# A shorter look-ahead for GpSimd's row fetches in a sparse two-layer graph kernel

## The chip, the cores and the metric

The kernel runs on one NeuronCore of a Trainium2 chip. The metric is the device time of one execution in microseconds. Engines are named as in the profile: PE is TensorE, DVE is VectorE, ACT is ScalarE, POOL is GpSimd, SP is the queue that issues plain DMAs.

## What is computed

Two graph layers over 2708 nodes with 512 features. `adj` is sparse (about 0.3% of its entries are set, values between 0.05 and 1) and has a nonzero diagonal.

```python
# layer 0
rowsum = adj.sum(axis=1)
d = where(rowsum > 0, rowsum ** -0.5, 0)
out = relu((d[:, None] * adj * d[None, :]) @ x @ W + b)
h = layernorm(x + out)
# layer 1
xn = h @ W_node + b_node
feats = einsum('nd,hdf->hnf', xn, K)          # 4 heads
logits = s[:, :, None] - 1e10 * (1 - adj)     # s: one number for each row and head
out = relu(mean over heads of softmax(logits) @ feats)
y = layernorm(h + out)
```

In layer 1 the factor 1e10 makes the softmax pick one column, that of the row's largest entry. So layer 1 needs, for row i, one row of `u = h @ M + c`, where `M` is the mean over heads of `W_node @ K`: the row of the largest entry of `adj[i]`. Rows where that would not hold exactly raise a flag, and a dense path stands behind the flag.

## The kernel before, in words

**Blocks and chunks.** Rows go in blocks of 128 (`NB` = 22; `NS` = 21 are whole). A first stage loads `adj`, sums its rows on ACT, finds the largest entries of each third of a row on DVE, and stores the scaled products `v = d * (x @ W)` to DRAM as `v_d`. The main loop then goes over blocks `ib` 0 to 20 and in each over `C` = 9 chunks `c`, with `n = 9 * ib + c`. Each chunk needs 128 rows of `v_d`, gathered by an indirect DMA of 256 KB that GpSimd issues (`fetch_chunk`, `fetch`, line 611). In chunks 0, 3 and 6 of a block the gathered rows are the rows' own largest entries of one third; in blocks 1 to 20 DVE adds them in (`add_chunk`, line 662). The other six chunks hold the rest of the entries in packed lists (`lists[ib]`, computed one block or more ahead by `hot`, `enlist` and `listed`), and PE adds them with a small 128x128 matrix (line 672).

**Order of work.** The schedule is by hand (`manual_schedule`): each engine does its instructions in the order in which the program writes them, and waits on semaphores only where data or buffers are not ready. So an instruction written earlier or later matters only by what it then stands before or behind on its own engine. Gather buffers are taken from two pools of 12 in turn (`row_space`, lines 617 to 622) once the search has ended, which is in block 8 (`found_at` = 8); so a buffer comes round again 24 gathers later.

**Look-ahead.** Ahead of chunk `n`, `fetch_until(m)` writes the gathers of all chunks below `m` that are not yet written, as far as their lists exist. Line 1151 gives `m`. The list of a block must have been written before its chunks 1, 2, 4, 5, 7 and 8 can be gathered; `fetch_until` stops at the first block without a list.

**The tail that is mixed in.** `norm_1` (lines 711 and 712, then `squares`, line 721) ends a block; its normalised rows `h` are turned on PE (`turn_h`), multiplied by `M` (`u_product`, line 235), read from PSUM by DVE into `ut` (line 790) and stored as `u`. Rows below 2304 (`EARLY` = 18 blocks) go to `u_e`, those of blocks 0 to 16 by a plain store on SP; block 17 by a scatter from GpSimd that leaves out flagged rows (`put`, line 1029, index `put_own`); later blocks by scatters into `u_d`. A few flagged rows are done by a dense sum (`l_a`, `l_v`, `acc_l`), and their product `l_u` is scattered into `u_e` (index `to_put`) and `u_d` (`put_d`) by two more `put`s. These three scatters are written at fixed distances in chunks after the products that they need (`later`).

Four chunks after the last row of `u_e` is written, `pieces_y(1)` follows in three chunks of four: `y_fetch(n)` gathers the selected rows of `u_e` for block n (line 1052, index `idx`), `y_1(n)` adds them to `h` on DVE six pieces later (line 1063, then `squares`), and in groups of three blocks come the root, the last normalisation and the store to `out`. After the main loop come the products of the last two blocks, the other `y` gathers, the rows whose selected row lies in `u_d` (index `top_d`) and their scatters to `out_dram` (line 1029). GpSimd has no other work in the main loop past block 10, except the root of the flagged rows (lines 268 to 271) and their two gathers.

**Where the change lies in the queue.** Among the last instructions on GpSimd of the main loop, in the order before: the gather of chunk (20,0), those of chunks (20,1) to (20,8), then `put` of `l_u` into `u_e`, `put` of block 17's `ut` into `u_e`, `put` of `l_u` into `u_d`, then `y_fetch` 0, 1, 2 and so on.

Of the kernel before, what the change touches and what calls it, by code (L numbers as in the profile page):

```python
# [44 lines left out]
ALU = mybir.AluOpType  # L45
# [18 lines left out]
def tile_two_graph_layers(  # L64
# [11 lines left out]
    nc = tc.nc  # L76
# [11 lines left out]
    def rows(ib):  # L88
        return min(P, N - ib * P)
# [60 lines left out]
    bad_i = const.tile([1, 1], I32, name="bad_i")  # L150
# [234 lines left out]
    def hot(ib):  # L385

        lo = max(g for g in GROUPS if g <= ib)
        ends = starts[lo]
        h_t = search.tile([P, T, 2 * P], BF16, name="hot", bufs=2)
        for t in range(T):  # L390
            past = search.tile([P, 2 * P], BF16, name="past", bufs=2)
            nc.vector.tensor_scalar(past, slots, ends[:, 1, ib - lo, t : t + 1], None, op0=ALU.is_gt)  # L392
            nc.vector.scalar_tensor_tensor(  # L393
                h_t[:, t, :], slots, ends[:, 0, ib - lo, t : t + 1], past, op0=ALU.is_gt, op1=ALU.subtract
            )
        hots[ib] = h_t

    def enlist(ib):
        ls = sheets[ib] = p_one.tile([P, D], F32, name="ls")
        h_t = hots.pop(ib)  # L400
        for k in range(NL):
            nc.tensor.matmul(
                ls[:, k * W_REC : (k + 1) * W_REC],
                h_t[:, k // 2, k % 2 * P : (k % 2 + 1) * P],
                packed[:, ib, k // 2, :],
                start=True,
                stop=True,
            )
# [36 lines left out]
    def search_next():  # L445
        ib, t = finds.pop(0)
        find(ib, t)
        if t == T - 1:
            under_0(ib)
            scanned[0] = ib + 1  # L450
            load_blocks()

    def group(lo):
        hi = GROUPS[GROUPS.index(lo) + 1]
        pack_1(lo, hi)
        pack_2(lo, hi)
        pack_3(lo, hi)
        if hi == NB:
            nc.vector.memset(flag[: N - full, NS:], 1.0)
# [40 lines left out]
    def weights(d):  # L500

        ps = p_po.tile([P, D], F32, name="po")
        for e in range(ND):
            nc.tensor.matmul(ps, wT[:, e, d * P : (d + 1) * P], km[:, e, :], start=(e == 0), stop=(e == ND - 1))
        nc.scalar.copy(m_sb[:, d, :], ps)
# [118 lines left out]
    def fetch_chunk(ib, c):  # L624
        kind, t = CHUNKS[c][:2]
        g = gs[ib, c] = row_space()
        if kind == "d":
            pr = rows(ib)
            fetch(g, pr, cols[:pr, ib, t, CHUNKS[c][2] : CHUNKS[c][2] + 1], v_d[: reach(c), :])
        else:  # L630
            fetch(g, P, lists[ib][0][:, t : t + 1], v_d[: reach(c), :])
# [25 lines left out]
    def add_chunk(ib, c):  # L657
        pr = rows(ib)
        g = gs.pop((ib, c))
        if by_vector(ib, c):  # L660
            vs = own[ib][0]
            nc.vector.scalar_tensor_tensor(  # L662
                vs, g, scaled[:, ib, CHUNKS[c][1], 0:1], vs, op0=ALU.mult, op1=ALU.add
            )
            return
        first = ib not in acc
        if first:
            acc[ib] = p_acc.tile([P, D], F32, name="acc")
            if bias_on_pe(ib):
                start_from(acc[ib], pr, b_3)  # L670
        k = pr if CHUNKS[c][0] == "d" else P
        nc.tensor.matmul(  # L672
            acc[ib][:pr],
            ss.pop((ib, c))[:k, :pr],
            g[:k],
            start=(first and not bias_on_pe(ib)),
            stop=(c == len(CHUNKS) - 1),
        )
# [60 lines left out]
    def root_1(lo, hi):  # L739

        s = slice(lo, hi)
        nc.scalar.activation(sds[:, s], sqs[:, s], AF.Sqrt, scale=1.0 / D, bias=eps_1)
        nc.vector.tensor_scalar(vrs[:, s], sqs[:, s], 1.0 / D, EPS, op0=ALU.mult, op1=ALU.add)
# [67 lines left out]
    def later(chunks_on, f):  # L811
        due.append([chunks_on, f])
# [295 lines left out]
    def fetch_until(n):  # L1108
        while fetched[0] < min(n, len(chunks)) and in_turn[fetched[0]][0] in lists:
            fetch_chunk(*in_turn[fetched[0]])  # L1110
            fetched[0] += 1

    def form_until(n):
        while formed[0] < min(n, len(chunks)) and chunks[formed[0]][0] in lists:
            small_matrix(*chunks[formed[0]])
            formed[0] += 1
# [28 lines left out]
    found_at = None  # L1145
    for ib in range(NS):
        pr = rows(ib)
        for c in range(C):
            n = ib * C + c
            form_until(n + 11)  # L1150
            fetch_until(n + (9 if n < 14 else 11) + (0 if found_at is None else min(11, max(0, 2 * (ib - found_at - 3)))))
            add_chunk(ib, c)
            group_of = max(g for g in GROUPS if g <= hot_next)
            if (
                c in (0, 5)
                and hot_next < NS
                and hot_next <= ib + (2 if c == 0 else 4)
                and group_of in starts
                and not (c == 5 and found_at is not None and ib == found_at + 1)
            ):  # L1160
                hot(hot_next)
                listing[n + 4] = lambda k=hot_next: enlist(k)
                listing[n + 6] = lambda k=hot_next: listed(k)
                hot_next += 1
            if n in listing:
                listing.pop(n)()
            if ib == 0 and c in (5, 8):
                weights(2 if c == 5 else 3)
            if finds and c in ((1, 4, 7) if ib < 3 else (1, 5)):
                search_next()  # L1170
            if c == 2 and not finds and found_at is None:
                group(GROUPS[2])
                searching[0] = False
                found_at = ib
            if found_at is not None:
                for f in plan.pop((ib - found_at, c), []):
                    f()
            if c == 2 and ib > ROOTS_AT:
                root_1(ib - 1, ib)
            if c == (2 if ib <= ROOTS_AT else 3) and ib:  # L1180
                k = slice(ib - 1, ib)
                if ib <= ROOTS_AT:
                    norm_2(ib - 1, ib, rows(ib - 1))
                else:
                    root_2(ib - 1, ib)
                    nc.scalar.activation(nbs[:, k], nms[:, k], AF.Copy, scale=rss[:, k])
                norm_3(ib - 1, rows(ib - 1), space(ib - 1))
                store(h_d, space(ib - 1), ib - 1)
                waiting_h.append(ib - 1)
            if c == (7 if ib < EARLY else 6):  # L1190
                for _ in range(2):
                    if waiting_h:
                        turn_h(waiting_h.pop(0))
            for k in sorted(products_u):
                u_store(k)
            if c == (5 if ib < EARLY else 8 if ib == EARLY else 1) or (ib == EARLY and c == 5):
                for k in sorted(hTs):
                    u_product(k)
            if found_at == ib - 3 and c == 4:
                products_l = list(range(NB))  # L1200
            if c % 2 and products_l:
                listed_turn(products_l.pop(0))
            elif len(dl.get("turned", [])) > (2 if products_l else 0):
                listed_product(dl["turned"].pop(0))
            if dl.get("at") == n - 2:
                root_1(L, L + 1)
                root_2(L, L + 1)
                norm_v(L, P, h_of[L])
                waiting_h.append(L)
            if L in h_of and "at" not in dl:  # L1210
                dl["at"] = n
            if "set" not in dl and u_done >= set(range(EARLY - 1)) | {L}:
                dl["set"] = n
                later(3, lambda: put(dl["u"], u_e[:, :], dl["put"][:, NLATE:], EARLY * P))
                later(5, lambda: put(dl["u"], u_d[:, :], dl["put_d"], N - EARLY * P))
            if "go" not in dl and u_done >= set(range(EARLY)) | {L}:
                dl["go"] = n + 4
            if n >= dl.get("go", n + 1) and (n - dl["go"]) % 4 != 3 and n < len(chunks) - 3:
                pieces_y(1)
            tick()  # L1220
        if not finds and late is None:
# [7 lines left out]
            po = p_po.tile([P, D], F32, name="po")  # L1229
# [13 lines left out]
    ib = NS - 1  # L1243
# [35 lines left out]
    po = p_po.tile([P, D], F32, name="po")  # L1279
# [14 lines left out]
    for n in first:  # L1294
        rows_out(n)
    root_2(second[0], second[-1] + 1)
    nc.vector.tensor_copy(bad_i, po[:1, :1])
    for n in second:
        y_3(n)
        rows_out(n)  # L1300
# [146 lines left out]
```

## Time and profile before

| | |
|---|---|
| time, median of 3 runs | 490.34 us (489.5 to 492.23) |
| the profiled execution's own time | 488.01 us |
| its span in the profile | 486.3 us |
| busy, share of the span: PE, DVE, ACT, POOL | 77%, 81%, 64%, 63% |
| DMA moved | 140.67 MB, mean 289 GB/s |
| gathers of line 611: lists, own entries | 126 at 1010 ns, 63 at 1007 ns |

The time lies 1.7 us above the span, which counts from the first to the last instruction. [...] Times in the views are microseconds from the span's start.

### The profile page before, as it was taken

To read this page: it belongs to the slowest core of one execution; us is meant where nothing else is said; L and a number is where in the kernel's file an instruction comes from. 1 tells how busy PE (TensorE), PEld (TensorE's weight loads), DVE (VectorE), ACT (ScalarE), POOL (GpSimd) and SP (SyncE) were. 2 spreads that over 40 slices of the span, in tenths; PEclk is the share of its full clock that TensorE was granted. 3 is DMA by queue.
4 is the path that set the end of the run, shared out by engine and by line. 5 is a ranking of instruction groups with operands and counts; after the bars stand their busy time and mean duration, and the time that the engine had idled before them with its cause. 6 is when DMAs were issued, how large, how long until landed. Compare 5 with 4: busy or idle time off the path is not lost.

```text
span 486.3 us, 5318 instructions
## 1 busy us (share of the span) xinstructions
PE 376.8 (77%) x1129; PEld 168.8 (35%) x1129; DVE 391.7 (81%) x1079; ACT 312.3 (64%) x575; POOL 305.3 (63%) x434
## 2 busy tenths in 40 slices
PE   4979788788978987799977958699999999880000
PEld 3434344333223333344323423344444444340000
DVE  2799989879799999999999996666667697667661
ACT  1599999797886556776773453865666322348680
POOL 2343544454477677777787577777777665677703
PEclk9998998798997999999999889799999999995555
DMA  7999999998548678889889789999999688469952
GB/s 232 419 398 416 422 339 371 357 336 342 197 119 286 202 235 264 263 253 315 272 258 290 228 261 371 376 325 376 369 367 313 219 270 269 138 194 308 322 193 84
DMA packets 51565, 140.67 MB, mean 289 GB/s; under 512 B 10617, under 2 KB 10617, under 8 KB 48688
## 3 DMA queue, kind: packets, MB, share of 16 engines
q0 software_dynamic: 21840, 68.29, 45.1%
q1 hardware_dynamic: 29684, 71.95, 39.4%
q8 instruction: 11, 0.18, 0.2%
q14 instruction: 30, 0.25, 0.2%
HBM read 117.33 MB, written 24.99 MB: 293 GB/s over the span
## 4 chain that ended last, share of the span: by engine, by line
DVE 28%; PE 19%; DMA 7%; issue 5%; ACT 3%; POOL 3%; POOLq 0%; DVEq 0%; ACTq 0%
PE acc L672 7%; PE po L235 6%; PE acc_l L1012 4%; DVE ats L319 4%; DVE vals L318 3%; DVE hot L393 3%; DVE vs L662 2%; DMA l_a<-in_adj_dram,to_read 2%; DMA g<-u_e,idx 2%; POOL g L611 1%; DVE past L392 1%; DVE h_early L712 1%; DMA g<-v_d,l_col 1%; DVE h_late L1063 1%; DVE vs L711 1%
## 5 line engine op out<-in xcount | busy, mean ns | idle before, releaser
L611 POOL DMA_INDIRECT g<-v_d,l_col x126 | 127.3, 1010 | 42.6 <-issue 22.1
L672 PE MATMUL acc<-g,s 128*128 128x512 f32 x278 | 143.2, 628 | 4.3 <-DMA g<-v_d,l_col 2.6
L235 PE MATMUL acc<-w_sb,sT 128*128 128x512 f32 (+1 forms) x176 | 89.1, 654 | 0.0
L235 PE MATMUL po<-m_sb,sT 128*128 128x512 f32 x176 | 80.8, 603 | 2.7 <-ACT sT L226 2.7
L611 POOL DMA_INDIRECT g<-v_d,cols x63 | 63.4, 1007 | 19.7 <-issue 13.1
L318 DVE MAX8 vals<-a 128x8 f32<-128x896 f32 (+2 forms) x66 | 71.7, 1087 | 2.8 <-ACT a L299 2.8
L319 DVE FIND_INDEX8 ats<-vals,a 128x8 uint32<-128x896 f32 (+2 forms) x66 | 72.1, 1092 | 0.0
L672 PEld LDWEIGHTS acc<-g,s 128*128 128x128 f32 x278 | 49.1, 196 | 50.1 <-issue 42.3
L305 ACT ACTIVATE a<-a 128x2708 f32<-128x2708 f32 (+1 forms) x22 | 54.4, 2471 | 12.4 <-DVE ats L319 12.4
L299 ACT ACTIVATE a<-a 128x2708 f32<-128x2708 f32 (+1 forms) x22 | 54.8, 2490 | 10.0 <-POOL a L311 10.0
L235 PEld LDWEIGHTS po<-m_sb,sT 128*128 128x128 f32 x176 | 33.5, 194 | 45.0 <-issue 38.2
L235 PEld LDWEIGHTS acc<-w_sb,sT 128*128 128x128 f32 (+1 forms) x176 | 34.7, 208 | 38.6 <-issue 38.5
L649 ACT ACTIVATE s<-s,l_val,l_minus 128x128 f32<-128x128 f32 x86 | 42.4, 493 | 2.9
L311 POOL TENSOR_SCALAR_AFFINE_SELECT a<-a 128x128 f32<-128x128 f32 (+1 forms) x22 | 7.2, 327 | 56.0 <-DMA a<-in_adj_dram 49.7
L226 ACT COPY sT<-tp 128x512 f32<-128x512 f32 (+1 forms) x44 | 25.8, 586 | 24.8 <-PE tp L224 24.8
L662 DVE SCALAR_TENSOR_TENSOR vs<-g,scaled,vs 128x512 f32<-128x512 f32 x50 | 37.2, 744 | 0.1
L224 PE MATMUL tp<-ident,x 128*128 128x128 f32 (+1 forms) x88 | 15.4, 303 | 23.6 <-DMA x<-in_x_dram 15.5
L648 ACT ACTIVATE s<-place,l_row 128x128 f32<-128x128 f32 x86 | 33.4, 388 | 0.0
L393 DVE SCALAR_TENSOR_TENSOR hot<-slots,ends,past 128x256 bf16<-128x256 bf16 x63 | 30.6, 485 | 2.2
L1052 POOL DMA_INDIRECT g<-u_e,idx x21 | 21.9, 1041 | 7.1 <-issue 5.5
L726 ACT ACTIVATE nms<-tot 128x1 f32<-128x1 f32 x10 | 2.0, 202 | 34.8 <-DVE h_early L712 19.5
L721 ACT ACTIVATE xr<-h_late,nms 128x512 f32<-128x512 f32 x11 | 7.9, 722 | 24.7 <-DVE nms L720 24.7
(265 smaller groups left out, 579.5 us busy)
## 6 DMA issues: line engine op xcount, KB each, us to landing
a<-in_adj_dram SPq DMA_DIRECT2D x21, 1354.0 KB, 9.3
x<-in_x_dram SPq DMA_DIRECT2D x21, 256.0 KB, 19.1
vs<-v_d SPq DMA_DIRECT2D x21, 256.0 KB, 4.9
xr<-in_x_dram SPq DMA_DIRECT2D x21, 256.0 KB, 5.9
l_v<-v_d SPq DMA_DIRECT2D x21, 256.0 KB, 5.0
u_e<-ut SPq DMA_DIRECT2D x17, 256.0 KB
h_d<-h_late SPq DMA_DIRECT2D x13, 256.0 KB, 2.9
out_dram<-h_late SPq DMA_DIRECT2D x13, 256.0 KB, 4.4
```

What stands on the lines that cost most here:

```text
L226: copy(sT[:, :, :pr], ps[:, :, :pr])
L235: nc.tensor.matmul(po[:pr], sT[:, f, :pr], wt[:, f, :], start=(f == 0 and row_3 is None), stop=(f == ND - 1))
L299: nc.scalar.activation(a, a, AF.Copy, accum_out=sums[:pr, ib : ib + 1])
L305: nc.scalar.activation(a, a, AF.Relu, scale=-1.0, accum_out=bad[:pr, NB + ib : NB + ib + 1])
L318: nc.vector.max(out=vals[:pr, ib, t, :], in_=part)
L319: nc.vector.max_index(out=ats[:pr, ib, t, :], in_max=vals[:pr, ib, t, :], in_values=part)
L393: nc.vector.scalar_tensor_tensor(h_t[:, t, :], slots, ends[:, 0, ib - lo, t : t + 1], past, op0=ALU.is_gt, op1=ALU.subtract)
L611: nc.gpsimd.indirect_dma_start(out=t[:pr], out_offset=None, in_=src, in_offset=bass.IndirectOffsetOnAxis(ap=ap, axis=0))
L648: nc.scalar.activation(s[:, :pr], place[:, :pr], AF.Abs, bias=minus_row[:, t : t + 1])
L649: nc.scalar.activation(s[:, :pr], s[:, :pr], AF.Relu, scale=minus_val[:, t : t + 1], bias=val[:, t : t + 1])
L662: nc.vector.scalar_tensor_tensor(vs, g, scaled[:, ib, CHUNKS[c][1], 0:1], vs, op0=ALU.mult, op1=ALU.add)
L672: nc.tensor.matmul(acc[ib][:pr], ss.pop((ib, c))[:k, :pr], g[:k], start=(first and not bias_on_pe(ib)), stop=(c == len(CHUNKS) - 1),)
```

## The change

Line 1151 no longer adds the term that grows with the block. With `found_at` = 8 it was 0 up to block 11, 2 in block 12, 4 in block 13 and so on up to 11, so that the nominal distance went from 11 to 22 chunks; what was really written ahead, because of the lists, was 16 to 22 chunks in blocks 16 to 18. Now it is 11 chunks everywhere. A second edit at line 1297 makes the flag by a comparison where it was a copy with a conversion; it is one operation on one element in both.

```diff
@@ -1148,7 +1148,7 @@
         for c in range(C):
             n = ib * C + c
             form_until(n + 11)
-            fetch_until(n + (9 if n < 14 else 11) + (0 if found_at is None else min(11, max(0, 2 * (ib - found_at - 3)))))
+            fetch_until(n + (9 if n < 14 else 11))
             add_chunk(ib, c)
@@ -1294,7 +1294,7 @@
     root_2(second[0], second[-1] + 1)
-    nc.vector.tensor_copy(bad_i, po[:1, :1])
+    nc.vector.tensor_scalar(bad_i, po[:1, :1], 0.0, None, op0=ALU.is_gt)
     for n in second:
```

The instructions of PE, DVE, ACT and SP keep their order. On GpSimd the order is the same up to the gather of chunk (20,0). From there it is:

```
before: (20,1) ... (20,8)   put l_u->u_e   put ut->u_e   put l_u->u_d   y0 y1 y2 y3 ...
after:  put l_u->u_e  (20,1)  put ut->u_e  (20,2)  put l_u->u_d  (20,3) (20,4) (20,5)
        y0 (20,6) y1 (20,7) y2 (20,8)  y3 ...
```

## Prediction

> **What bounds the kernel now.** I read the page first, then the chain of waits over the last 100 us, then the timelines of POOL, DVE and PE there. The page says that no engine is full over the whole span, but GpSimd's gathers are many and evenly long:
>
> ```profile
> L611 POOL DMA_INDIRECT g<-v_d,l_col x126 | 127.3, 1010 | 42.6 <-issue 22.1
> ```
>
> From 289 to 381 us POOL's timeline is one gather every 1.25 us (0.95 busy and 0.30 between) with hardly a wait. As a gather waits only for its list, its buffer and its turn, and the buffers are the same 24, writing it 11 chunks later in the program changes nothing in time as long as POOL has nothing else in between. That is so until chunk (20,0). What counts is the stretch where other GpSimd work is reordered. POOL's timeline there (start, busy time, what, and the idle time before it with its releaser):
>
> ```profile
> 395.83 0.95 POOL L611 DMA_INDIRECT g<-v_d,cols  x1 [0.30 <-PE acc L672]
> 398.62 0.95 POOL L611 DMA_INDIRECT g<-v_d,l_col  x1 [1.85 <-DVE l_val L438]
> ...
> 407.89 0.94 POOL L611 DMA_INDIRECT g<-v_d,l_col  x1 [0.30 <-issue]
> 409.13 1.02 POOL L1029 DMA_INDIRECT u_e<-l_u,to_put  x1 [0.30 <-DVE ut L790]
> 414.19 0.99 POOL L1029 DMA_INDIRECT u_e<-ut,put_own  x1 [4.04 <-DMA h_d<-h_late]
> 415.49 1.25 POOL L1029 DMA_INDIRECT u_d<-l_u,put_d  x1 [0.30 <-issue]
> 417.74 1.05 POOL L1052 DMA_INDIRECT g<-u_e,idx  x1 [1.00 <-DMA u_e<-ut,put_own]
> 419.10 1.03 POOL L1052 DMA_INDIRECT g<-u_e,idx  x1 [0.30 <-issue]
> 420.43 0.99 POOL L1052 DMA_INDIRECT g<-u_e,idx  x1 [0.30 <-issue]
> 421.73 1.01 POOL L1052 DMA_INDIRECT g<-u_e,idx  x1 [0.30 <-issue]
> ```
>
> The reader is to see the eight gathers (20,1) to (20,8) from 398.62 to 408.83, the three scatters, and y0 to y3 from 417.74. After that POOL issues one DMA every 1.3 us without a wait until 461.58. The page names a store of `h` as what ended the 4.04 us; the wait itself, on POOL's sequencer, lies between 407.25 and 413.15 and ends with the landing of the scatter of 409.13, since both write `u_e`.
>
> The chain of waits shows that this queue sets the end:
>
> ```profile
> 414.19 2.74 DMA u_e<-ut,put_own
> ...
> 420.43 3.71 DMA g<-u_e,idx
> ...
> 426.42 3.71 PE po L235 x8
> ...
> 450.99 6.04 DMA g<-u_e,idx
> 457.05 0.71 DVE h_late L1063 x2
> ```
>
> It goes through the scatter, y2, then PE's product of block 19, DVE's work on `y`, and again through POOL: the gather of y17, issued at 450.99, lands at 457.02, and DVE has idled 2.41 us for it. So a delay of POOL's queue beyond y3 reaches the end in full, and a delay of DVE alone only beyond 2.41 us.
>
> **The change part by part.**
>
> The flag edit: the copy is one DVE instruction of 0.14 us at 475.31; the comparison is taken at the same. Nearest rows are 128x1 operations of 0.14 to 0.20 us, so between 0 and +0.06 us, and the last scatters wait for other things. I take 0.
>
> The look-ahead in blocks 12 to 20, up to chunk (20,0): no instruction of any engine changes place. 0.
>
> The reordering. I follow POOL from 397.08 (end of (20,0) plus 0.30).
>
> 1. The scatter of `l_u` now stands first. It needs `l_u`, which DVE writes until 403.35, and the landing of block 16's plain store into `u_e`, issued on SP at 402.06. POOL's sequencer waited for that store from 402.73 to 406.56; it was hidden, as gathers were already queued ahead. Now nothing covers it. The store took 4.5 us among five gathers in flight; the store of `h` at 412.03, with little beside it, took 2.0. So the scatter starts between 404.2 and 406.7; I take 405.3, as the gathers that crowded the store are now behind it. POOL's wait: 8.2 us, where before it waited 1.55 for the list (1.85 less 0.30).
>
> 2. One gather (1.31 us, the eight took 10.51) follows. Then block 17's scatter needs the first scatter's landing and `ut`. The landing took 4.0 us behind eight gathers; the second scatter landed in 2.74 with little ahead. With 1.07 us from landing to start (413.12 to 414.19) that gives 405.3 + 2.74 + 1.07 = 409.1, up to 411.5 from the late end. `ut` of block 17 is the other bound:
>
> ```profile
> 402.66 0.69 DVE L790 TENSOR_TENSOR l_u<-po,c_bc 128x512 f32<-128x512 f32 x1 [0.62 <-PE po L235]
> 408.25 0.69 DVE L790 TENSOR_TENSOR ut<-po,c_bc 128x512 f32<-128x512 f32 x1 [0.89 <-PE po L235]
> ```
>
> It ends at 408.94 and comes from a PE product that nothing here touches, so 409.0 is the floor. I take 409.5.
>
> 3. From there POOL has no reason to wait: two scatters (1.30 and 1.55), seven gathers (7 x 1.31 = 9.17) and y0 to y2 (1.36, 1.33, 1.30), 16.0 us up to y3. y0's need, the landing of the second scatter, comes at about 412.3, well before its turn. Starts: y0 417.6 (before 417.74), y1 420.3 (419.10), y2 422.9 (420.43), (20,8) 424.2 (407.89), y3 425.5 (421.73). So everything on POOL from y3 on is 3.8 us later; 3.3 at the floor, 5.8 at the other end.
>
> 4. Chunks (20,7) and (20,8) are no longer ready. They landed at 411.98 and 412.95 and were used here:
>
> ```profile
> 418.56 2.74 PE L672 MATMUL acc<-g,s 128*128 128x512 f32 x6
> 422.53 1.88 PE L672 MATMUL acc<-g,s 128*128 128x512 f32 x4
> ```
>
> The earlier ones still come in time: (20,1), issued at 406.6, lands by 411 and is used at 414.27; (20,2) to (20,5), issued between 410.8 and 416, land some 3.5 us later, about when they are used (418.56 to 420.7). (20,8), issued at 424.2, lands at 427.7 with y2's quiet 3.7 or y0's 3.24 us (4.6 is the median under load), and PE is done with it at 428.6. DVE's sum of block 20 (line 711) started at 425.81, held by y2 and not by PE; it now starts at 428.6: +2.8. PE's product of block 19 stands behind the same matmul, at 426.42 before and 428.6 now: +2.2. So block 20's chain and DVE's `y` work are late by 2.2 to 2.8 us.
>
> 5. At y17 DVE arrives 2.5 us later, the gather lands 3.8 us later by POOL. The later one wins: 3.8. A little comes back: the stores to `out`, which shared the DMAs with this 6.04 us landing (DMA share 0.95 between 450 and 460), are late by DVE's 2.5 only, so up to 1.3 us of them is out of the way; I take 0.3 of it. The sum is +3.5 us.
>
> By the profiled execution, 488.01 + 3.5 = 491.5. That execution lies 2.3 us under the median of the runs, and I put the sum on the median: 490.34 + 3.5 = 493.8.
>
> [...]
>
> **The rivals.**
>
> A. The shift is mostly absorbed (no change that can be measured). If the late `out` stores free the DMAs fully, y17 lands in 4.6 instead of 6.04 us and comes 3.3 - 1.4 = 1.9 us late, as DVE is 2.2 late: +2.2, 492.5. For it: only 2.41 us of DVE's idle time hang on that landing. Against: POOL's floor of +3.3 is firm.
>
> B. The late end: the store's landing stays at 4.5 us and the first scatter's at 4.0. Then POOL is late by 5.8, (20,8) lands at 429.7 or later, and block 20 is late by 4 to 5. +5.8, 496.1. For it: both landings are what was measured. Against: the crowd of gathers behind which they stood is gone.
>
> C. Faster: the gathers fill the scatters' waits. Before, POOL idled 4.04 + 1.00 us on landings, less 0.30 each; after, gathers stand between the scatters, and if the scatters' inputs were there on arrival at 397, these 4.4 us would be saved and the tail would start that much sooner: -4.4, 485.9. It decides if `l_u` and `ut` of block 17 are ready before about 405; DVE's rows put them at 403.35 and 408.94, after POOL's arrival.
>
> D. The change doesn't reach the chip's timing at all, because POOL's order is the same: excluded for the tail, where the order differs, and assumed for the blocks before.
>
> **How the numbers follow.** The main case (+2.8 to +4.6) has 0.55, A 0.20, B 0.20, C 0.05, D none. About 0.5% (2.45 us) is what a measurement of this kernel tells from no change: 487.9 to 492.8. A and a small part of no other case lie inside it. So slower 0.75, same 0.20, faster 0.05. The range takes in A's end with the runs' own scatter (the lowest run lies 0.8 under the median) and B's with theirs: 490.9 to 497.5.
>
> **What would show it.** Right: POOL's row of the first scatter at 404 to 407 with 7 to 10 us idle before it, the second at 409 to 411, y3 at 425 to 428, and the `vs` sum of block 20 near 428.6. Wrong: y3 before 424, or y3 late and the last scatters to `out` not, which would mean that DVE or the DMAs set the tail; or any difference before 395 us.

## Result and profile after

The changed kernel takes 491.74 us (median of 20 runs, 490.32 to 494.04), the kernel before 489.6 us in the same comparison (20 runs, 487.9 to 492.23). The ratio is 1.0038 [1.0024, 1.0052]: slower by about 0.4%, 2.1 us. (The ratios here, with a 95% interval, leave out executions more than 1.5% above the kernel's fastest, and need not equal the quotient of two medians.) The profiled execution of the changed kernel took 491.33 us, with a span of 489.6 us: 3.3 us more than the first profile of before.

POOL's timeline of the changed kernel, in the stretch where its queue was reordered (start, busy time, what, idle time before it and its releaser):

```profile
404.86 1.02 POOL L1029 DMA_INDIRECT u_e<-l_u,to_put  x1 [8.24 <-DVE vs L700]
...
409.07 1.01 POOL L1029 DMA_INDIRECT u_e<-ut,put_own  x1 [1.91 <-DVE s L653]
...
416.86 1.03 POOL L1052 DMA_INDIRECT g<-u_e,idx  x1 [0.30 <-issue]
...
423.73 1.02 POOL L611 DMA_INDIRECT g<-v_d,l_col  x1 [0.30 <-issue]
425.05 1.02 POOL L1052 DMA_INDIRECT g<-u_e,idx  x1 [0.30 <-issue]
```

The scatter of `l_u`, which now stands first, begins after 8.24 us of waiting; the second scatter is where its floor was (`ut` of block 17 ends at 408.78 here); y3 (the last row) is issued at 425.05, where before it was at 421.73. POOL's queue is late by 3.32 us there, and by 3.68 at y17.

PE's timeline, first of the kernel before and then of the changed one, shows what becomes of chunks (20,7) and (20,8), which are the two `acc` rows, and of the product of block 19 behind them:

```profile
422.53 1.88 PE L672 MATMUL acc<-g,s 128*128 128x512 f32 x4
426.42 3.70 PE L235 MATMUL po<-m_sb,sT 128*128 128x512 f32 x8 [2.00 <-ACT sT L226]
```

```profile
425.59 1.10 PE L672 MATMUL acc<-g,s 128*128 128x512 f32 x2 [3.09 <-DMA g<-v_d,l_col]
428.20 2.05 PE L672 MATMUL acc<-g,s 128*128 128x512 f32 x2 [1.52 <-DVE h_early L1063]
430.04 5.34 PE L235 MATMUL po<-m_sb,sT 128*128 128x512 f32 x8
```

PE stands 3.09 and 1.52 us, and then the eight matmuls of the product take 5.34 us where before they took 3.70. (The view puts the second wait down to DVE's row of y2, which ended just then; but the gather of (20,8) lands at 428.07, and before, the same matmuls ran ahead of y2's row. The wait is for that gather.) The reason for the longer product is in the windows, two of the kernel before and three of the changed one (stretch; its length; busy time and instructions of PE, PEld, DVE, ACT and POOL; granted PE clock; DMA share; GB/s):

```profile
425.00:430.00 5.00, 3.58 (x9) 1.62 (x10) 2.25 (x6) 2.39 (x6) 3.78 (x5) 1.00 0.64 178
430.00:435.00 5.00, 3.90 (x25) 2.74 (x24) 3.90 (x17) 2.05 (x6) 4.00 (x4) 1.00 0.64 200
```

```profile
420.00:425.00 5.00, 1.80 (x7) 0.61 (x5) 2.13 (x10) 2.63 (x6) 3.83 (x4) 1.00 0.68 197
425.00:430.00 5.00, 2.89 (x4) 1.08 (x5) 1.51 (x4) 1.29 (x3) 4.04 (x4) 0.67 0.69 200
430.00:435.00 5.00, 5.00 (x9) 2.11 (x9) 1.54 (x4) 1.11 (x3) 3.78 (x5) 0.65 0.61 190
```

The granted clock falls to half from 426.7 to 433.5; before, it was 1.00 in all of these windows. DVE pays for both, in its timeline, first before and then changed:

```profile
425.81 0.69 DVE L711 TENSOR_TENSOR vs<-acc,vs 128x512 f32<-128x512 f32 x1
...
430.15 0.69 DVE L790 TENSOR_TENSOR ut<-po,c_bc 128x512 f32<-128x512 f32 x1 [2.73 <-PE po L235]
...
457.05 0.69 DVE L1063 SCALAR_TENSOR_TENSOR h_late<-g,h_late 128x512 f32<-128x512 f32 x1 [2.41 <-DMA g<-u_e,idx]
```

```profile
430.29 0.69 DVE L711 TENSOR_TENSOR vs<-acc,vs 128x512 f32<-128x512 f32 x1 [1.28 <-PE acc L672]
...
435.42 0.69 DVE L790 TENSOR_TENSOR ut<-po,c_bc 128x512 f32<-128x512 f32 x1 [3.52 <-PE po L235]
...
459.88 0.69 DVE L1063 SCALAR_TENSOR_TENSOR h_late<-g,h_late 128x512 f32<-128x512 f32 x1
...
461.63 0.69 DVE L1063 SCALAR_TENSOR_TENSOR h_late<-g,h_late 128x512 f32<-128x512 f32 x1 [0.41 <-DMA g<-u_e,idx]
```

The sum of block 20 is 4.48 us later than before, `ut` of block 19 5.27 us later. At y17 (459.88) DVE has no idle time before it any more, where it had 2.41 us: its own chain arrives when the gather lands (459.86). y18, the last row shown, waits 0.41 for its landing. From there every row is 3.3 us late, to the end.

The chain of waits of the changed kernel now goes through the slowed product and then through POOL again:

```profile
422.41 5.02 DMA g<-u_e,idx
428.20 2.05 PE acc L672 x2
430.25 5.15 PE po L235 x8
...
445.32 4.84 DMA g<-u_e,idx
```

### The profile page after: what moved, and what is told of

Same layout as the page of the kernel before. It is cut to its first block, busy times and chain, and to the rows that moved or that the text cites. A ratio compares the mean times of both kernels' runs of the same rounds, so it can differ in the third digit from the quotient of the medians.

```text
span 489.6 us, 5315 instructions
## 1 busy us (share of the span) xinstructions
PE 382.0 (78%) x1129; PEld 170.4 (35%) x1129; DVE 393.1 (80%) x1079; ACT 312.3 (64%) x575; POOL 306.3 (63%) x434
## 4 chain that ended last, share of the span: by engine, by line
DVE 24%; PE 23%; DMA 7%; ACT 4%; issue 4%; POOL 3%; POOLq 0%; DVEq 0%
PE acc L672 9%; PE po L235 8%; PE acc_l L1012 4%; DVE ats L319 3%; DMA g<-u_e,idx 3%; DVE vals L318 3%; DVE hot L393 2%; DVE vs L662 2%; DMA l_a<-in_adj_dram,to_read 2%; POOL g L611 2%; DVE h_early L712 1%; DMA g<-v_d,l_col 1%; DVE past L392 1%; DVE vs L711 1%; DVE s L653 1%
## 5 line engine op out<-in xcount | busy, mean ns | idle before, releaser
L672 PE MATMUL acc<-g,s 128*128 128x512 f32 x278 | 148.9, 651 | 8.5 <-DMA g<-v_d,l_col 5.3
L235 PE MATMUL po<-m_sb,sT 128*128 128x512 f32 x176 | 84.8, 628 | 0.7 <-ACT sT L226 0.7
L235 PE MATMUL acc<-w_sb,sT 128*128 128x512 f32 (+1 forms) x176 | 84.9, 628 | 0.0
L672 PEld LDWEIGHTS acc<-g,s 128*128 128x128 f32 x278 | 50.7, 202 | 56.8 <-issue 46.9
L235 PEld LDWEIGHTS po<-m_sb,sT 128*128 128x128 f32 x176 | 35.3, 204 | 46.2 <-issue 41.1
L235 PEld LDWEIGHTS acc<-w_sb,sT 128*128 128x128 f32 (+1 forms) x176 | 33.2, 199 | 35.7 <-issue 35.6
L711 DVE TENSOR_TENSOR vs<-acc,vs 128x512 f32<-128x512 f32 x20 | 13.7, 685 | 13.6 <-PE acc L672 13.6
```

The costliest lines, as they stand in the source:

```text
L235: nc.tensor.matmul(po[:pr], sT[:, f, :pr], wt[:, f, :], start=(f == 0 and row_3 is None), stop=(f == ND - 1))
L672: nc.tensor.matmul(acc[ib][:pr], ss.pop((ib, c))[:k, :pr], g[:k], start=(first and not bias_on_pe(ib)), stop=(c == len(CHUNKS) - 1),)
```

## The experiments

**A measure that leaves out the start.** In the profiles of both orders block 16's sum on DVE (line 711) starts anywhere between 377.4 and 380.0 us; that spread comes from the stages before the change. So the table counts from that row; its times come from one profile of each kernel. "End" is the end of the last instruction on any engine; "gap" is DVE's idle time right before y17; "halved" is for how long the granted clock was at half before 440 us; "product" is PE's time for block 19.

| kernel | ratio to before | y3 issued | product | halved | y17 issued | gap | end |
|---|---|---|---|---|---|---|---|
| before, first profile | 1 | 43.94 | 3.70 | 0 | 73.20 | 2.41 | 102.20 |
| e2, before's order | 1.0008 [0.9987, 1.0029] | 44.02 | 5.40 | 3.4 | 73.70 | 1.39 | 102.89 |
| e13, before again | 0.9989 [0.9967, 1.0011] | 44.84 | 5.93 | 6.8 | 75.44 | 0.00 | 104.75 |
| changed | 1.0038 [1.0024, 1.0052] | 47.42 | 5.34 | 6.8 | 77.04 | 0.00 | 105.64 |
| e4, look-ahead alone | 1.0050 [1.0030, 1.0070] | 47.47 | 5.17 | 6.8 | 76.94 | 0.70 | 105.44 |
| e14, changed again | 1.0028 [1.0005, 1.0051] | 47.35 | 5.36 | 6.8 | 77.01 | 0.70 | 105.84 |
| e1, look-ahead 17 | 0.9979 [0.9954, 1.0004] | 44.20 | 3.70 | 0 | 73.60 | 1.75 | 101.89 |
| e3, look-ahead 14 | 1.0044 [1.0024, 1.0064] | 46.56 | 5.17 | 3.4 | 76.47 | 0.42 | 104.99 |
| e9, changed, late rows last | 1.0027 [1.0005, 1.0049] | 47.36 | 5.61 | 6.8 | 71.76 | 0.00 | 105.05 |
| e10, changed, PE kept busy | 1.0039 [1.0015, 1.0063] | 47.73 | 3.70 | 0 | 78.14 | 3.58 | 106.34 |
| e11, changed, both | 1.0003 [0.9974, 1.0031] | 47.44 | 3.70 | 0 | 71.31 | 0.00 | 102.79 |
| e12, before, both | 0.9961 [0.9938, 0.9984] | 44.83 | 3.70 | 0 | 69.84 | 0.00 | 101.33 |
| e15, before, late rows last | 0.9962 [0.9930, 0.9995] | 44.83 | 5.40 | 3.4 | 69.56 | 0.00 | 102.82 |
| e16, before, PE kept busy | 0.9962 [0.9943, 0.9982] | 44.83 | 3.70 | 0 | 74.32 | 2.23 | 103.44 |

### How far ahead, and from which block

Three kernels keep 11 chunks up to block 17 and then take 17, 22 or 14; the flag is as before.

```diff
-            fetch_until(n + (9 if n < 14 else 11) + (0 if found_at is None else min(11, max(0, 2 * (ib - found_at - 3)))))
+            fetch_until(n + (9 if n < 14 else 11 if found_at is None or ib < 18 else 17))
```

**e1, 17 chunks.** Six gathers stand ahead of the first scatter, and the other two behind it.

> Look-ahead 11 up to block 17, then 17; flag edit undone. Six gathers now stand ahead of the scatter of l_u, one between the first two scatters, one between the second and the third, none behind. Theory P (GpSimd's queue sets the end, and its waits for inputs are what the order moves): the six gathers fill the wait for block 16's store; the first scatter starts at about 406.5 us, the second at 411, y3 at 419.5 (before 421.73, changed kernel 425.05), and the end moves with it: 2 us faster than before, ratio 0.996. Rival D (DVE, ACT and the stores to out set the tail in most executions, and GpSimd's place matters only when it is late): y3 as early, but the end at most 0.5 us sooner, ratio 0.999 to 1.000.

Measured: 488.47 us against 490.16, not told apart from before. The queue is not sooner: POOL's timeline of e1,

```profile
405.17 0.94 POOL L611 DMA_INDIRECT g<-v_d,cols  x1 [0.30 <-issue]
409.37 1.48 POOL L1029 DMA_INDIRECT u_e<-l_u,to_put  x1 [3.26 <-DVE s L653]
```

has the first scatter 2.9 us later than expected. The store of block 16 into `u_e`, for which it waits, was issued at 401.84 as ever and landed at 407.21, 5.37 us later, where it took 2.08 us in the changed kernel. So the expectation had the store landing too soon: the six gathers put ahead of the scatter move on the DMAs beside it (from 400 to 410 us packets took 85% of the 16 DMA engines' time in e1, and 45% in the changed kernel), which is the likely reason. The other 2.1 us, from the landing to the scatter's start, are not explained (see the end).

**e2, 22 chunks from block 18.** This is before's order of instructions on every engine.

> Look-ahead 11 up to block 17 as in the changed kernel, then 22 as before; flag edit undone. Every engine then has the order of before. If only the order behind chunk (20,0) matters, ratio 1.000 within 0.15%, and the profile is a second execution of before: the first scatter near 409 us, y3 near 421.7. If the shorter look-ahead in blocks 12 to 17 costs or gains by itself, ratio as for the changed kernel, 1.004. Its profile also tells whether the first profile of before was a quick execution: by its span against 486.3 us.

Measured: 490.17 us against 490.16. So the growing look-ahead of blocks 12 to 17 is worth nothing that these runs can tell (1.0008 [0.9987, 1.0029]), as the prediction said, and what the change costs lies in the order behind chunk (20,0). But the profile differs from the first one of before, with the same instructions in the same order. PE's timeline of e2:

```profile
428.00 5.40 PE L235 MATMUL po<-m_sb,sT 128*128 128x512 f32 x8 [2.14 <-ACT sT L226]
```

PE stood 2.14 us here, 2.00 in the first profile; here the clock was halved for 3.4 us and the product took 5.40 us. The first profile of before was a quick one in this very stretch.

**e3, 14 chunks.** Three gathers ahead of the first scatter.

> Look-ahead 11 up to block 17, then 14; flag edit undone. Three gathers ahead of the scatter of l_u; the last gather stands right before y0, so none stands between the y gathers. Theory P: first scatter still at 404.9 us (its input sets it), second at 409.1, y3 at 421.3, as before within 0.4 us; the last chunk lands in time; ratio 0.999. If the cost of the changed kernel lies in the scatters coming early and not in what stands behind them, it stays slow, ratio 1.004.

Measured: 491.62 us against 490.16, as slow as the changed kernel; the expectation was missed. POOL's timeline of e3:

```profile
407.75 1.03 POOL L1029 DMA_INDIRECT u_e<-l_u,to_put  x1 [5.26 <-DVE vs L662]
```

The store was issued at 402.30 and landed at 406.88, 4.58 us later. With none, three, six and eight gathers ahead of the scatter its landing takes 2.1 (changed, e4), 4.6, 5.4 and 4.3 to 4.8 us (the six profiles with before's order of these instructions). It does not grow with each gather, but in none of these eight profiles with gathers about was it short: here the wait was not filled for nothing. So an instruction's place matters also by the transfers it puts beside others, and not only, as said ahead of the prediction, by what it stands before or behind on its own engine. Counted from block 16's sum, the scatter starts 2.5 us later than in the changed kernel (29.71 against 27.23) for 3.9 us of gathers got out of the way, and y3 gains 0.9 us.

### The flag

**e4** makes only the edit of line 1151; the flag stays a copy.

> The look-ahead edit alone, flag edit undone. Ratio 1.004 as the changed kernel's 1.0038, if the flag edit costs nothing; 1.000 if the flag edit is what costs. Its profile is a second one of the changed order: y3 at 425, block 20's sum on DVE 3 to 5 us late; whether PE's clock halves again in the wait for chunks (20,7) and (20,8) (0.5 from 426.7 to 433.5 us in the first profile) is to be seen. If it does not, DVE's y work should be 0.8 us or more earlier against the same point, and the end unmoved, as y18's landing holds it.

Measured: 492.04 us against 490.16, ratio 1.0050 [1.0030, 1.0070], which takes in the changed kernel's 1.0038. The cost is the look-ahead's, and none of the flag's can be told.

### Two bounds at y17

The changed profile has DVE's chain and the gather arrive at y17 together. Theory: two bounds lie there, POOL's queue (+3.3 us) and PE's halved clock, which holds DVE back; taking one away shows the other, and only both together bring the time back. Two edits, each alone and both together, and both on the kernel before. The first writes the reads of the late rows (`late_h`, gathers on POOL) behind the last `y` gathers, so that y17 is issued four gathers sooner:

```diff
-    for k in range(NLATE):
-        late_h(k)
     u_store(ib)
     ys[L] = row_space()
     fetch_some(ys[L], dl["top"][:, NLATE:], u_e[:, :], EARLY * P)
     y_ahead(NS)
+    for k in range(NLATE):
+        late_h(k)
```

The second gives PE transposes of the identity to do, whose result nothing reads, while it would stand: in the changed order in block 20,

```diff
+            if ib == NS - 1 and c == 7:
+                stir(10)
...
                         turn_h(waiting_h.pop(0))
+                if ib == NS - 1:
+                    stir(22)
```

and in the kernel before ahead of block 19's product, where it stood about 2 us in the first profile and in e2:

```diff
     ib = NS - 1
+    stir(14)
     u_product(ib - 1)
```

These four kernels ran twice. The first time the kernel before itself took 536.31 us, and the ratios decide nothing: 1.0080 [1.0030, 1.0131], 1.0151 [1.0091, 1.0212], 1.0113 [1.0048, 1.0178] and 1.0001 [0.9952, 1.0051] for e5 to e8; what made all of them slow stays open.

> The changed kernel with the four gathers of late rows (from h_d, 5.2 us of GpSimd) moved behind the y gathers, so that y17 to y20 are issued and land about 5 us sooner. Theory T (in the changed kernel two bounds meet at y17: its landing at 459.9 us, and DVE's chain through block 20 that arrives at 459.8): DVE no longer waits at y17 and y18 (0.4 to 0.7 us), so the end comes 0.4 to 0.7 us sooner; ratio to before 1.003 (the changed kernel: 1.004 to 1.005). Rival Q (the queue alone): 3 us or more sooner, ratio 0.998 or less. Rival D (DVE's chain alone): ratio as the changed kernel's.

> The changed kernel with idle transposes on PE in its two waits in block 20: 22 of them before chunk (20,7), 10 before (20,8), which fill the 3.1 and 1.5 us in which PE stood. If the halved clock (0.5 from 426.7 to 433.5 us) comes from that standing, it is now full, PE's product of block 19 takes 3.6 instead of 5.3 us, and DVE's y work from y3 on is 2.5 us sooner. Theory T and rival Q: the end hardly moves (0 to 0.3 us), since y17's landing stays; DVE now waits about 2.5 us there; ratio 1.004. Rival D: the end moves by 2.5 us, ratio 0.999. If the clock halves all the same, the standing was not the cause, and nothing moves.

> Both edits of e5_late_rows_last and e6_pe_warm on the changed kernel. Theory T: only together do they move the end, by 2.5 to 3 us against the changed kernel: ratio to before 0.998 to 0.999. Rival Q: as e5 alone. Rival D: as e6 alone.

> The kernel before with the late rows' gathers moved behind the y gathers, and 14 idle transposes on PE ahead of block 19's product (2 us of standing there). DVE no longer waits 1.4 to 2.4 us at y17, and where the clock halved at 428 us (the second profile of this order) 1.8 us of PE and DVE come back. Theory T: 2 to 3 us faster than before, ratio 0.994 to 0.996, and the times lie closer together. Rival Q: the same or a little less, 0.995. Rival D: by the clock alone, 0.997.

The second time, with the kernel before at 490.13 us:

**e9, changed order, late rows last.**

> The kernel of e5_late_rows_last again, since there the kernel before itself took 536 us. Theory T (landing of y17 and DVE's chain meet at y17 in the changed kernel): 0.4 to 0.7 us sooner than the changed kernel, ratio to before 1.003. Rival Q (queue alone): 3 us sooner, 0.998 or less. Rival D (DVE's chain alone): 1.004 to 1.005.

Measured: 491.26 us. y17 is issued 5.3 us sooner after block 16 than in the changed kernel, and the end only 0.6 us: DVE does not wait at y17, as its own chain is just as late. POOL's queue alone is not what holds y17.

**e10, changed order, PE kept busy.**

> The kernel of e6_pe_warm again. If PE's standing is what halves its clock, block 19's product takes 3.6 instead of 5.3 us and DVE's y work from y3 on is 2.5 us sooner. Theory T and rival Q: DVE waits for y17 and the end hardly moves, ratio 1.004. Rival D: 0.999.

Measured: 491.93 us, no gain. The clock stays full, the product takes 3.70 us and `ut` of block 19 starts 2.4 us sooner; then DVE's timeline of e10 has

```profile
460.80 0.69 DVE L1063 SCALAR_TENSOR_TENSOR h_late<-g,h_late 128x512 f32<-128x512 f32 x1 [3.58 <-DMA g<-u_e,idx]
```

at y17: all that PE won, DVE waits for the gather, which is issued 1.1 us later than in the changed kernel besides (why is not shown).

**e11, changed order, both.**

> The kernel of e7_both again: both edits on the changed kernel. Theory T: only together do they move the end, by 2.5 to 3 us, ratio to before 0.998 to 0.999. Rival Q: as the late rows' move alone. Rival D: as the warm PE alone.

Measured: 489.64 us, ratio 1.0003 [0.9974, 1.0031], a little above the 0.998 to 0.999 expected and within the interval; the end is 2.85 us sooner than in the changed kernel (102.79 against 105.64), where the two edits alone gave -0.6 and +0.7; the three profiles of the changed order lie within 0.4. PE's timeline of e11, the clock full throughout:

```profile
423.65 2.56 PE L244 MATMUL po<-ident 128*128 128x128 f32 x22
...
430.72 3.70 PE L235 MATMUL po<-m_sb,sT 128*128 128x512 f32 x8 [0.48 <-ACT sT L226]
```

That is the shape of two bounds that meet, and the theory stands; one profile of each kernel carries it, as the times alone hardly part e9 from e11.

**e12, before with both edits.**

> The kernel of e8_before_both again: before, with the late rows' gathers last and 14 idle transposes ahead of block 19's product. Theory T: 2 to 3 us faster than before, 0.994 to 0.996. Rival Q: 0.995 to 0.997. Rival D: 0.997.

Measured: 488.20 us against 490.13, faster than both kernels, and the soonest end of all the profiles (101.33). Which of the two edits does it is asked by e15 and e16 below.

### How steady the two orders are

**e13** is the kernel before once more, **e14** the changed kernel once more.

> The kernel before once more, for another profile. If the first profile was a quick execution, this one looks like that of e2_ahead22_late: clock halved near 428 us, block 19's product 5.4 us, y17 gathered 73.7 us after block 16's sum and the end 102.9 us after it (first profile: 73.2 and 102.2). If the first was typical, the clock is full and the end 102.2 us after. Ratio 1.000.

> The changed kernel once more. Ratio 1.0044 (between 1.0038 and 1.0050); in the profile the end 105.5 us after block 16's sum, so 2.6 us more than a usual execution of before, and the clock halved from 426 to 433 us as in both profiles of this order. A ratio of 1.007 would say that the prediction's 3.5 us was right and the 20 runs were not typical.

Measured: 490.70 and 491.47 us (the kernel before beside them 490.26). e14's end is the expected one; its ratio, 1.0028 [1.0005, 1.0051], is below the 1.0038 to 1.0050 expected, which its interval takes in. e13's end is not as expected: 104.75, where about 103 was expected. PE's timeline of e13:

```profile
431.37 5.93 PE L235 MATMUL po<-m_sb,sT 128*128 128x512 f32 x8 [4.80 <-ACT sT L226]
```

In this execution of before, PE stood 4.80 us, the clock was halved for 6.8 us, and DVE had no idle time left at y17. The clock is the smaller part of that. Counted from block 16's sum, the product ends 5.0 us later than in the first profile: 2.2 are its own slowness and 2.8 the longer pause. PE's pause ends when y2 has landed and DVE and ACT have worked on it; y2 was issued 0.9 us later and took 5.57 us to land, where it took 3.70 in the first profile and 3.73 in e2. So in before's order both the landings and the clock vary from one execution to the next (ends of 102.20, 102.89 and 104.75, mean 103.28); the clock was halved in all four profiles of the changed order without the transposes (e9's is the fourth), and the three ends of the unedited order lie close (105.64, 105.44 and 105.84, mean 105.64). The difference of the means, 2.36 us, is near what the medians show (2.1), as near as three profiles 2.5 us apart can tell; the difference of the first two profiles, 3.4, is not typical.

**e15 and e16** are the two edits of e12 one at a time.

> The kernel before with only the late rows' gathers moved behind the y gathers. Theory T: y17 lands 5 us sooner, DVE's chain decides, and the end comes 1.4 us sooner where the clock halves (2.4 where not): ratio 0.996 to 0.997. Rival Q: 0.990. Rival D: 1.000.

> The kernel before with only the 14 idle transposes ahead of block 19's product. Theory T: the product takes 3.7 us, DVE's chain is up to 1.8 us sooner and waits that much longer for y17; the end does not move, ratio 0.999 to 1.000. Rival D: 0.996.

Measured: 489.44 and 489.60 us, ratios 0.9962 [0.9930, 0.9995] and 0.9962 [0.9943, 0.9982]. e15's ratio came as expected; its end, 102.82, is 0.5 us sooner than the mean of before's three profiles, where 1.4 to 2.4 were expected. e16 was expected to be worth nothing, since the first profile of before has 2.41 us of DVE's idle time at y17. In e13 there is none, and there a full clock could pay; but that is not shown, as e16's own profile has 2.23 us idle there and ends no sooner than that mean (103.44 against 103.28). By the medians both gains are under 0.2%. The three ratios of e12, e15 and e16 can't be told apart; the end in the profiles (101.33 against 102.82 and 103.44) speaks for the two together.

## Why the prediction was right or wrong

**Right: the queue.** The first scatter was put at 405.3 and came at 404.86 after 8.24 us of idle time (8.2); the second at 409.5 and 409.07; y0, y1, y2, chunk (20,8) and y3 at 417.6, 420.3, 422.9, 424.2 and 425.5, and they came at 416.86, 419.46, 422.41, 423.73 and 425.05. Step 1's choice of the store's landing, about 2 us without the gathers and not 4.5 with them, is what made this good, and e3 and e1, where gathers stand ahead again, have it at 4.6 and 5.4. The second scatter lies on its floor and y3 is late by 3.3, the floor's figure. The flag is worth nothing that can be told (e4), nor is the look-ahead before block 18 (e2). Of the four signs named for being right, three came; the fourth, block 20's sum near 428.6, did not (430.29).

**Wrong: step 4, block 20.** The prediction put PE's end of (20,8) at 428.6 and block 20 late by 2.8. PE ended at 430.25. Of the 1.65 us missed, 0.4 is the landing of (20,8), 428.07 and not 427.7; the other 1.3 are PE's, which needed 2.2 us from the landing and not 0.9: its last two matmuls took 2.05 us, where four took 1.88 before. No term of the sum had the PE clock in it: the step asked when PE would get its data, and not what standing for it does to the work that follows. The product of block 19 then cost 1.6 us more. Block 20 was late by 4.48 and `ut` by 5.27, where the main case had 2.8 at most (B had 4 to 5, by a later landing and not by the clock).

**Step 5 was right by luck, with two errors.** The prediction had DVE 2.5 us late at y17, with POOL deciding alone. DVE was 5.24 late by its own chain: 2.41 us of cover gone and 2.83 more. By just these 2.83 the gather was late too: 3.68 at the issue, less 0.85 in the landing (5.19 in place of 6.04 us), where 0.3 was allowed. With y18's 0.41 the end moved by 3.28 in the first pair of profiles; the sum had said 3.5. The waits meet, so neither error showed in the end, and the profiled execution even took 491.33 us, where the sum on the first profile had said 491.5. e10 and e9 each free one side to find the other at once.

**The step that failed for the time** is "I put the sum on the median". The prediction saw that its execution lay 2.3 us under the median, and still took a difference against it, +3.5, for one against the median. That execution was quick in the stretch that the change rewrites: the clock full in the product, PE's pause 2.00 us where e13 has 4.80, and POOL's wait ahead of the second scatter 4.04 us where e13 has, as it happens, 4.80 too. Its end lies 1.1 us ahead of the mean of three profiles of that order. Against an ordinary execution the shift is 2.36 us by the profiles and 2.1 by the medians. With the median of the first three runs 0.74 us above that of the twenty, this is the whole miss of 2.1 us: 493.8 - 491.74 = 2.06, and 0.74 + (3.5 - 2.14) = 2.10. The +3.5 itself measured +2.1.

**A slip in the working that decided nothing.** The range's ends do not follow from what is said of them: A's 492.5 less 0.8 is 491.7, not 490.9.

**The rivals.** A had +2.2 us, which is the size measured, and not the reason: it wanted the landing of y17 down to 4.6 us and DVE 2.2 late, and they were 5.19 and 5.24. (By its own numbers it had +1.9, as 2.2 of DVE's lateness lie within the 2.41 of cover.) What is absorbed is that before's own order often pays a longer pause and the halved clock as well. B, with the store's landing at 4.5 us, is refuted for the change (2.08); e3 and e1 brought that landing about, by other orders. C, the gathers in the scatters' waits, was said to hang on `l_u` and `ut`; e1 and e3 add that the filling itself delays the store. D held for the blocks before 18, as assumed (e2), and not for the tail.

## What to carry to other kernels

In a queue that issues in the program's order, as GpSimd's does here, look not only at what a wait can be filled with but at what is waited for: the store that ended this wait took 2.1 us to land with no gathers put ahead of the scatter, and 4.3 to 5.4 us with three to eight. When a change makes PE stand, look at the clock granted afterwards, and cost the next work at that rate: in the changed kernel, where PE stood 3.09 and then 1.52 us, it was 0.50 from 426.7 to 433.5, and the product took 5.34 us in place of 3.70. And before adding a difference to a median, take a second profile of the kernel before, or look whether the stretch in question carries its run-to-run spread.

## What the runs showed of the hardware

**The PE clock.** Ahead of block 19's product PE stood 2.00 us in the first profile of before and 2.46 in e1, and the clock stayed full; it stood 2.14 in e2, 3.52 in e15 and 5.15 in e3, and the clock was halved for 3.4 us; 4.80 in e13, and 3.1 to 3.2 and then 0.6 to 1.5 in the changed order, and it was halved for 6.8. In e10 and e11 transposes fill most of the pauses, and in e12 and e16 the first 1.69 us of some 3.7 (PE still stood 2.08 and 2.01 us behind them); the clock stayed full. So the length of a pause alone does not decide: the clock stayed full behind 2.46 us in e1 and was halved behind 2.14 in e2. What else decides is not shown.

Up to 440 us the profile of before has the granted clock at 0.50 eight times, five times for 3.41 us and three times for 6.83; that of the changed kernel has it so ten times, six times for 3.41 us, three times for 6.83 and once for 10.24.

**Open.** In e1 POOL's sequencer was through its wait at 407.24 and the scatter started at 409.37, 2.1 us later; in the changed kernel (404.02 to 404.86) and in e3 (406.91 to 407.75) it took 0.8. No run tells why. Nor does any tell what makes the landings vary from one execution to the next.
